# Two adjacency walks of a graph layer done as 2x2 blocks with seven products

## The chip, the cores and the metric

One core of one Trainium2 chip. The metric is the device time of one execution in microseconds; each kernel is given as the median of its runs. The profile is of one further execution, whose own time stands beside its span. Engine names in the profile: PE is TensorE (matmuls), PEld its loads of the stationary operand, DVE is VectorE, ACT is ScalarE, POOL is GpSimd, SP is SyncE, which here issues DMAs.

## The reference

Two graph layers over N = 2708 nodes with D = 256 features, all in float32; `adj` is a dense 2708 x 2708 matrix, mostly zeros. Only layer 0 matters for the change:

```python
R = adj + eye(N);  R = R / R.sum(-1, keepdims=True)
Xf = Xa = X;  Z = 0
for n in range(2):
    A  = top_p_attention(Xa, W1, W2, W3)   # softmax rows, cut at 0.9 of their mass
    Xf = R @ Xf
    Xa = A @ Xa
    Z  = Z + Xf @ U1[n].T + Xa @ U2[n].T
x = layernorm(X + layernorm(X + Z) * g + b)
```

Layer 1 is a graph attention with four heads over the mask `adj != 0`, a residual and a layer norm.

## The kernel before, in words

The rows are cut into 22 tiles (`rows`): 16 of 128 and 6 of 110. `adjT`, the transposed adjacency, lies in DRAM.

`fast_layer0` does layer 0. It has two attention steps (`step(0)`, `step(1)`) and two "walks", the products with R. By Horner's rule the walks run on projected features: `terms1` makes X U1[0].T (kept in DRAM as `c1`) and X U1[1].T (kept in SBUF as `xe`, with a column of ones for the row sums). Walk 0 multiplies R by `xe` and adds `c1`, giving `xm`; walk 1 multiplies R by `xm` and gives Xf's whole share of Z. The identity in R is added by VectorE when a row is done (`xf` at L931, `xw` at L990), not in the matrix.

One row of a walk is 22 matmuls (L917), one for each source tile j: the stationary operand is the 128 x 128 block of `adjT`, the moving one the 256 features (257 in walk 0) of the source tile, all summed in one PSUM bank (`ps_wk`, one buffer). The blocks come as half rows of 11 tiles (`blk`, three buffers in `adjp`, loaded two ahead by SP).

`step(s)` goes through the 22 row tiles of an attention step. For each row it has six groups of source tiles, and for each group one **slot**: four transposes of the score row `e` (`turned`, L256, into `ps_tr`, two buffers), ScalarE's copy (`eT`, L261), and four matmuls with the features (L274). The transposes of group n+1 stand before the matmuls of group n. After each group `slot(spend)` advances the searches for the cut of later rows (`going`: `scores`, `survey`, `bound`, `candidates`, `settle`, mostly VectorE and GpSimd; the last instruction of a search on VectorE is L851, the final `e`), then whatever finishes rows (`doing`), then the walks by `spend` matmuls:

```python
owed[0] += spend
while owed[0] > 0:
    owed[0] -= 1
    if next(stream, True):
        break
```

The search for row t + 3 is begun in the fifth slot of row t. In step 0 the spend is zero. Between the steps it is SPEND_BETWEEN per slot, 15 slots and those that `doing` needs, while the first searches of step 1 run; in step 1 it is SPEND_1. So walk 0 lies in the gap and the first part of step 1, walk 1 in the rest. All order is written out by hand (`manual_schedule`): each engine takes its instructions in program order, and waits on others by semaphores alone. `after_walk0` scales a row of walk 0 and adds `c1` (GpSimd); `finish` scales a row of walk 1, adds the other terms, and does two layer norms and layer 1's projections (`norms`, `sources`) in the slots that follow. Walk 1 waits in the program until no row of walk 0 is unfinished.

`layer1` follows: per source tile two loads of mask rows and features, VectorE's weights (`pt`, L1306) and TensorE's sums (L1318, L1328). `settle` there adds `xe`, the result of layer 0.

Of the kernel before, what the change touches and what calls it, by code (L numbers as in the profile page):

```python
# [8 lines left out]
F32 = mybir.dt.float32  # L9
# [27 lines left out]
SPEND_BETWEEN, SPEND_1 = 7, (7, 6, 7, 7, 6, 7)  # L37
# [8 lines left out]
def kernel(  # L46
# [55 lines left out]
    xe = const.tile([P, NT, D + 1], F32, name="xe")  # L102
    nc.gpsimd.memset(xe[:, :, D : D + 1], 1.0)
# [9 lines left out]
    vd = [kept.tile([P, D], F32, name=f"v_{t}") for t in range(NT)]  # L113
    bad = const.tile([1, 1], I32, name="bad")
# [41 lines left out]
    def sources(t, pool, room, queue=nc.sync):  # L156

        m = rows[t]
        tp = room()
        for c in range(DC):  # L160
            nc.tensor.transpose(tp[:, c, :m], xe[:m, t, c * P : (c + 1) * P], ident[:m, :m])
        xT = pool.tile([P, DC, P], F32, name="xT")
        nc.scalar.copy(xT[:, :, :m], tp[:, 0:DC, :m])
        yield
        wp = room().rearrange("p a b -> p (a b)")
        for c in range(DC):
            nc.tensor.matmul(  # L167
                wp[:m, : D + 2 * H], xT[:, c, :m], wx[:, c, :],
                start=(c == 0), stop=(c == DC - 1),
            )  # L170
        nc.scalar.activation(sb[:m, t, :], wp[:m, D : D + H], AF.Exp)
        nc.scalar.activation(tj[:m, t, :], wp[:m, D : D + H], AF.Exp, scale=NEG_SLOPE - 1.0)
        nc.scalar.copy(s_src[:m, t, :], wp[:m, D + H : D + 2 * H])
        vt = pool.tile([P, D], F32, name="cs")
        for h in range(H):
            cols = slice(h * FO, (h + 1) * FO)
            nc.scalar.activation(
                vt[:m, cols], wp[:m, cols], AF.Copy, scale=sb[:m, t, h : h + 1]
            )
        queue.dma_start(vd[t][:m], vt[:m])  # L180

    def norms(t, xt):

        m = rows[t]
        hh = xe[:m, t, 0:D]
        yield from layernorm(hh, hh, m)
        nc.gpsimd.tensor_mul(hh, hh, g_sb[:m])
        nc.gpsimd.tensor_add(hh, hh, xt[:m])
        yield
        yield from layernorm(hh, hh, m)  # L190
        yield
        yield
# [90 lines left out]
    def general_layer0():  # L283
        with ExitStack() as l0:
# [6 lines left out]
            load_x(xe)  # L291
            nc.scalar.dma_start(w1_sb, w1T.rearrange("(c p) e -> p c e", p=P))
# [248 lines left out]
    def fast_layer0(ep, adjp):  # L541
# [9 lines left out]
        )  # L551
        ps_lg, ps_wk, ps_at, ps_tr = (
            l0.enter_context(tc.tile_pool(name=name, bufs=bufs, space=PSUM))
            for name, bufs in (("ps_lg", 2), ("ps_wk", 1), ("ps_at", 1), ("ps_tr", 2))
# [66 lines left out]

        def query_weights():

            tr = ps_tr.tile([P, 4, P], F32, name="tr")
            for c in range(DC):
                nc.tensor.transpose(tr[:DA, c, :], w1_raw[:, c, :], ident)
            nc.vector.tensor_copy(w1_sb, tr[:DA, 0:DC, :])
            for c in range(DC):
                tr = ps_tr.tile([P, 4, P], F32, name="tr")
                nc.tensor.matmul(  # L630
                    tr[:, 0, :DA], w1_sb[:, c, :], w2_sb, start=True, stop=True
                )
                nc.vector.tensor_copy(wkqk[:, c, 1], tr[:, 0, :DA])
# [235 lines left out]

        def walks():  # L870

            queue = [
                (s, t, j0, j1)
                for s in range(STEPS) for t in range(NT) for j0, j1 in ((0, HT), (HT, NT))
            ]

            def load(s, t, j0, j1):  # L880
                m = rows[t]
                blk = adjp.tile([P, NT - HT, P], F32, name="blk")
                if (s, t) < (0, 2):

                    nc.gpsimd.memset(blk[:, :, 0:1], 0.0)
                by_tile(blk[:, :, :m], adjT[:, off[t] : off[t + 1]], j0, j1)
                return blk

            blocks = [load(*queue[0]), load(*queue[1])]
            yield  # L890
            for n, (s, t, j0, j1) in enumerate(queue):
                m = rows[t]
                cur, w = (xe, D + 1) if s == 0 else (xm, D)
                while s and unfinished:
                    yield True
                blk = blocks.pop(0)
                if n + 2 < len(queue):
                    blocks.append(load(*queue[n + 2]))
                if j0 == 0:
                    ac = ps_wk.tile([P, CHUNK], F32, name="walk")  # L900
                    if s and t >= NT - LATE:
                        ca = x_late[:, t - NT + LATE, :]
                        nc.gpsimd.memset(ca[:, 0:1], 0.0)
                    else:
                        ca = finp.tile([P, D], F32, name="ca", bufs=4)
                    if s:
                        cb = finp.tile([P, D], F32, name="cb")
                        nc.sync.dma_start(ca[:m], x[off[t] : off[t + 1], :])
                        nc.sync.dma_start(cb[:m], c2[t][:m])
                        if t in c3:  # L910
                            assert t in stored
                            held[t] = finp.tile([P, D], F32, name="cc")
                            nc.sync.dma_start(held[t][:m], c3[t][:m])
                    else:
                        nc.sync.dma_start(ca[:m], c1[t][:m])
                for j in range(j0, j1):
                    nc.tensor.matmul(  # L917
                        ac[:m, :w], blk[: rows[j], j - j0, :m], cur[: rows[j], j, 0:w],
                        start=(j == 0), stop=(j == NT - 1),
                    )  # L920
                    if j == NT - 1:
                        doing.append(after_walk0(t, ac, ca) if s == 0 else finish(t, ac, ca, cb))
                        next(doing[-1])
                    yield j == NT - 1

        def after_walk0(t, ac, ca):
            m = rows[t]
            unfinished.add(t)
            r = rinv[:m, t : t + 1]
            xf = rowp.tile([P, D + 1], F32, name="xf")  # L930
            nc.vector.tensor_add(xf[:m], ac[:m, : D + 1], xe[:m, t, :])  # L931
            nc.vector.reciprocal(r, xf[:m, D : D + 1])
            yield
            nc.gpsimd.tensor_scalar(xf[:m, :D], xf[:m, :D], r, None, op0=ALU.mult)
            nc.gpsimd.tensor_add(xm[:m, t, :], xf[:m, :D], ca[:m])
            unfinished.remove(t)
# [3 lines left out]
        def after_attention0(t, xa):  # L940
# [7 lines left out]
            tp = ps_tr.tile([P, 4, P], F32, name="tr")  # L948
            turn(xa, m, tp, nc.scalar.copy, xT)
            yield  # L950
            if t % 2:
                pj = ps_tr.tile([P, 4, P], F32, name="tr").rearrange("p a b -> p (a b)")
                project(1, off[t - 1], 2 * m, pj, both, nc.scalar.copy, nc.scalar.copy)
                yield
            terms2(t, xT)

        def terms1(t, xT):

            m = rows[t]
            cy = ps_tr.tile([P, 4, P], F32, name="tr").rearrange("p a b -> p (a b)")  # L960
# [7 lines left out]
            nc.scalar.copy(xe[:m, t, 0:D], cy[:m, D : 2 * D])  # L968
            nc.gpsimd.dma_start(c1[t][:m], cs[:m])

        def terms2(t, xT):

            m = rows[t]
            cy = ps_tr.tile([P, 4, P], F32, name="tr").rearrange("p a b -> p (a b)")
# [10 lines left out]
        def finish(t, ac, ca, cb):  # L985

            m = rows[t]
            xt = xe[:m, t, 0:D]
            xw = rowp.tile([P, D], F32, name="xw")[:m]
            nc.vector.tensor_add(xw, ac[:m, :D], xm[:m, t, :])  # L990
            yield
            nc.scalar.activation(xw, xw, AF.Copy, scale=rinv[:m, t : t + 1])
            while t not in held:
                yield
            nc.gpsimd.tensor_add(xt, ca[:m], cb[:m])
# [3 lines left out]
            if t < NT - LATE:  # L999
                yield  # L1000
                yield from norms(t, ca)
                yield from sources(t, rowp, lambda: ps_tr.tile([P, 4, P], F32, name="tr"))
# [3 lines left out]
        early = []  # L1006
        ready, held = {}, {}
        stream = walks()
# [7 lines left out]
        def slot(spend, begin=None):  # L1016
# [5 lines left out]
            advance(doing)  # L1022
            owed[0] += spend
# [5 lines left out]
        def step(s, cur, spend):  # L1029
            turned_first = None  # L1030
            for t in range(NT):
# [3 lines left out]
                if s == 0 and t == NT - 1:  # L1035
                    next(stream)
                if s and t == NT - 2:
                    share(0, ps_tr.tile([P, 4, P], F32, name="tr"))
# [4 lines left out]
                def between(n):  # L1043
# [11 lines left out]
                    if s and (t, n) == (NT - 1, len(groups) - 2):  # L1055

                        early.extend(neighbours(0, j, adjp) for j in first[:2])
                    slot(spend[n], (s, t + 3) if n == len(groups) - 2 else None)
# [55 lines left out]
        with tc.manual_schedule(engines=engines):  # L1114
            query_weights()
            ahead = turn_x(groups[0])
            for n in range(len(groups)):
# [3 lines left out]
                pj = ps_tr.tile([P, 4, P], F32, name="tr").rearrange("p a b -> p (a b)")  # L1121
# [9 lines left out]
            layer1_weights()  # L1131
            step(0, xm, [0] * len(groups))
# [80 lines left out]
    def layer1(ep, adjp, r=None, verdict=None, early=()):  # L1213
# [61 lines left out]

        if r is None:
# [92 lines left out]
        def beside(g, i):  # L1369
# [6 lines left out]
            for part in list(running):  # L1376
                if next(part, running) is running:
                    running.remove(part)
            if rest and i >= 2 and i % 2 == 0:
# [119 lines left out]
```

## Time and profile before

| | |
|---|---|
| median of 3 runs | 1572.68 us (1571.36 to 1573.06) |
| the profiled execution: time, span | 1571.97 us, 1570.2 us |
| granted TensorE clock | 0.994 |
| step 0 / gap / step 1 with walk 0 / step 1 with walk 1 | 71 to 441 / 441 to 515 / 515 to 808 / 808 to 1194 us |
| the walks' matmul records, L917 | 2 x 968, 447 us |
| the attention's, L274 | 2 x 968, 462 us |
| DMA | 128.40 MB, 82 GB/s on average |

A float32 matmul shows as two records. In the table of groups a row reads: line, engine, operation, output<-inputs, shapes, count | busy us, mean ns of one | idle time of the engine before them and what ended most of it. Matmul records overlap, so the mean of one is longer than its pace. In the list of waits a row reads: who waited <- for whom: us in total, times, longest.

### The profile page before, as it was taken

Reading aid. Unit: us, or ns where it says so; the run is one execution under the profiler, and the core shown is the slowest. Engines: PE = TensorE matmul, PEld = TensorE weight load, DVE = VectorE, ACT = ScalarE, POOL = GpSimd, SP = SyncE. Lnnn points to the kernel's source line nnn. Section 1 sums busy time; section 2 is a strip of 40 time slices with the busy share of each in tenths; the row PEclk is TensorE's granted clock in tenths of the full one; section 3 lists DMA queues with packets and bytes.
Section 4 is the critical chain, followed back from the end, with each engine's and each line's share of the span. In section 5 each row is a group of like instructions: output and inputs, shape, how many; then the busy total and the mean of one; then the engine's idle time right before and its main releaser. Section 6 shows DMA issues by size and latency. Waiting matters only on the chain.

```text
span 1570.2 us, 25877 instructions
## 1 busy us (share of the span) xinstructions
PE 1531.9 (98%) x9085; PEld 1034.5 (66%) x9085; DVE 1207.4 (77%) x3689; ACT 792.7 (50%) x1428; POOL 410.8 (26%) x853
## 2 busy tenths in 40 slices
PE   8999999999998999999999999999999999999995
PEld 4477777776776888887787788887778323333342
DVE  4686777677308876878769888888885898999995
ACT  3444444444345355555555556556552444456474
POOL 2200000001022122232224454534542120035143
PEclk9999999999999999999999999999999999999998
DMA  6100000000144343333334343333335335334331
GB/s 165 61 12 13 9 13 9 9 9 11 45 103 117 86 101 82 97 79 74 86 87 108 94 111 104 105 102 100 100 76 140 101 107 173 107 101 133 85 109 45
DMA packets 172501, 128.40 MB, mean 82 GB/s; under 512 B 44342, under 2 KB 161804, under 8 KB 172362
## 3 DMA queue, kind: packets, MB, share of 16 engines
q1 hardware_dynamic: 162553, 112.36, 27.2%
q0 software_dynamic: 3648, 9.26, 1.8%
q10 hardware_dynamic: 6161, 5.03, 1.0%
q8 instruction: 74, 1.21, 0.3%
q14 instruction: 65, 0.53, 0.1%
HBM read 111.78 MB, written 13.46 MB: 80 GB/s over the span
## 4 chain that ended last, share of the span: by engine, by line
PE 88%; DVE 7%; issue 1%; POOL 1%; ACT 1%; DMA 0%; ACTq 0%; DVEq 0%; POOLq 0%
PE att L274 25%; PE walk L917 24%; PE acc L1318 11%; PE lg L677 7%; PE tr L256 6%; PE acc L1328 6%; DVE pt L1306 3%; PE tr L962 2%; PE tr L976 2%; PE tr L647 1%; PE tr L167 1%; DVE scr L767 1%; DVE scr L848 0%; DVE cand L782 0%; DVE e L851 0%
## 5 line engine op out<-in xcount | busy, mean ns | idle before, releaser
L261 ACT COPY eT<-tr 128x512 f32<-128x512 f32 (+5 forms) x264 | 141.4, 536 | 280.9 <-PE tr L256 278.3
L702 ACT ACTIVATE junk<-e,minus,rth 128x2708 bf16<-128x2708 f32 (+1 forms) x88 | 232.9, 2646 | 36.1 <-POOL rth L734 35.2
L274 PE MATMUL att<-xm,eT 128*128 128x256 f32 (+3 forms) x968 | 230.9, 380 | 0.4 <-ACT xa L1047 0.4
L274 PE MATMUL att<-ba,eT 128*128 128x256 f32 (+3 forms) x968 | 230.9, 380 | 0.3 <-ACT eT L261 0.2
L917 PE MATMUL walk<-xe,blk 128*128 128x257 f32 (+3 forms) x968 | 225.3, 384 | 5.0 <-DVE xf L931 5.0
L917 PE MATMUL walk<-xm,blk 128*128 128x256 f32 (+3 forms) x968 | 222.0, 380 | 1.5 <-DVE xw L990 1.5
L1318 PE MATMUL acc<-pt,v 128*32 128x512 f32 (+3 forms) x2112 | 218.3, 543 | 4.1 <-DVE pt L1306 3.2
L917 PEld LDWEIGHTS walk<-xe,blk 128*128 128x128 f32 (+3 forms) x968 | 178.5, 187 | 50.3 <-issue 12.6
L917 PEld LDWEIGHTS walk<-xm,blk 128*128 128x128 f32 (+3 forms) x968 | 177.6, 186 | 35.1 <-issue 4.9
L1306 DVE SCALAR_TENSOR_TENSOR pt<-e,tj,blk 128x1024 f32<-128x1024 f32 (+3 forms) x176 | 184.3, 1112 | 11.8 <-PE att L274 8.7
L274 PEld LDWEIGHTS att<-xm,eT 128*128 128x128 f32 (+3 forms) x968 | 169.6, 186 | 22.1 <-ACT xa L1047 0.8
L274 PEld LDWEIGHTS att<-ba,eT 128*128 128x128 f32 (+3 forms) x968 | 169.5, 186 | 22.1 <-ACT eT L261 0.8
L681 ACT ACTIVATE e<-lg 128x1024 f32<-128x1024 f32 (+1 forms) x132 | 121.1, 922 | 110.5 <-PE lg L677 107.0
L1318 PEld LDWEIGHTS acc<-pt,v 128*32 128x32 f32 (+1 forms) x2112 | 68.9, 110 | 138.3 <-issue 110.5
L782 DVE MAX8 cand<-e 128x8 f32<-128x170 f32 (+1 forms) x352 | 89.6, 323 | 90.5 <-ACT e L681 90.4
L256 PEld LDWEIGHTS tr<-ident,e 128*128 128x128 f32 (+3 forms) x968 | 115.1, 138 | 56.3 <-issue 21.0
L256 PE MATMUL tr<-ident,e 128*128 128x128 f32 (+3 forms) x968 | 147.1, 271 | 0.7 <-ACT xe L968 0.3
L1328 PE MATMUL acc<-pt,sb 128*32 128x512 f32 (+3 forms) x1056 | 113.0, 542 | 0.0
L1306 DVE SCALAR_TENSOR_TENSOR pt<-r,tj,blk 128x1024 f32<-128x1024 f32 (+1 forms) x88 | 109.9, 1313 | 1.2 <-PE acc L1328 0.4
L237 ACT ACTIVATE blk<-blk 128x1024 f32<-128x1024 f32 (+3 forms) x66 | 63.3, 959 | 79.3 <-DMA blk<-in_adjT_dram 63.9
L782 DVE MAX8 cand<-scr 128x8 f32<-128x97 f32 (+1 forms) x616 | 102.2, 244 | 0.0
L931 DVE TENSOR_TENSOR xf<-walk,xe 128x257 f32<-128x257 f32 (+1 forms) x22 | 9.4, 426 | 110.9 <-PE walk L917 110.9
(235 smaller groups left out, 1959.3 us busy)
## 6 DMA issues: line engine op xcount, KB each, us to landing
blk<-in_adjT_dram SPq DMA_DIRECT2D x32, 704.0 KB
blk<-in_adjT_dram SPq DMA_DIRECT2D x32, 512.0 KB
blk<-in_adjT_dram SPq DMA_DIRECT2D x48, 330.0 KB
blk<-in_adjT_dram SPq DMA_DIRECT2D x32, 320.0 KB
blk<-in_adjT_dram SPq DMA_DIRECT2D x12, 605.0 KB
blk<-in_adjT_dram SPq DMA_DIRECT2D x12, 440.0 KB
blk<-in_adjT_dram SPq DMA_DIRECT2D x18, 283.6 KB
c<-cs POOLq DMA_DIRECT2D x32, 128.0 KB, 2.0
```

The lines of the kernel that those rows point to most:

```text
L237: nc.scalar.activation(bar, bar, AF.Sign)
L256: nc.tensor.transpose(tr[: rows[t], q, :m], e[:m, off[t] : off[t + 1]], ident[:m, :m])
L261: copy(eT[:k, : len(grp), :m], tr[:k, : len(grp), :m])
L274: nc.tensor.matmul(acc, eT[: rows[t], q, :m], value(t), start=(t == 0), stop=(t == NT - 1),)
L677: nc.tensor.matmul(lg[:m, h, :w], qT[part, cols], kT[s][part, c0 : c0 + w], start=True, stop=True,)
L681: nc.scalar.activation(halves[:m, :, c0 : c0 + w], lg[:m, :, :w], AF.Exp, accum_out=zp[:m, n : n + 1],)
L702: nc.scalar.activation(junk[:m], e[:m], func, scale=rth, bias=minus1[:m], accum_out=acc)
L782: nc.vector.max(cand[:, n, :], src[:m, n * size : min(N, (n + 1) * size)])
L917: nc.tensor.matmul(ac[:m, :w], blk[: rows[j], j - j0, :m], cur[: rows[j], j, 0:w], start=(j == 0), stop=(j == NT - 1),)
L1306: nc.vector.scalar_tensor_tensor(pt[:k, :gw], targets[g][h // 2][:k, h % 2, :gw], tj[:k, j, h : h + 1], bar, op0=ALU.max, op1=ALU.mult,)
L1318: nc.tensor.matmul(acc[h // 2][c][to : to + SIDE, :w], v[j][:k, h, o : o + SIDE], probs[n][h][:k, c0 : c0 + w], **at,)
L1328: nc.tensor.matmul(acc[2][c][h * SIDE : (h + 1) * SIDE, :w], sb[:k, j, h : h + 1].to_broadcast([k, SIDE]), probs[n][h][:k, c0 : c0 + w], **at,
```

## The change

Row tiles and source tiles are taken in pairs (11 of each, i and j), the features in halves of 128. In each pair of pairs the 2x2 block product is done with seven products instead of eight (Winograd's form of Strassen's scheme). On the side of the adjacency:

- S1 = A21 + A22, S2 = S1 - A11, S3 = A11 - A21, S4 = A12 - S2; D11 and D22 are A11 and A22, in which the identity is added into the diagonal block.

On the side of the features: T3 = B22 - B12, T2 = T3 + B11, T1 = B12 - B11, T4 = B21 - T2.

**Sums of the adjacency** (`mixes`): in step 0's slots, nine slots per row pair, 11 row pairs. SP loads the four blocks (each 11 x 128 x 128), GpSimd makes two diagonal adds and four sums in three pieces each, SP stores six blocks to DRAM. The fourth and fifth buffer are one tile of `wk`.

**The walks**: a row pair is seven phases of 11 matmuls with 128 moving columns (129 in the first three phases of walk 0); each phase's block is one load of 704 KB, two phases ahead. Two PSUM banks alternate, so `ps_tr` falls to one buffer, and the other small users of `ps_tr` take the banks of the walks before these begin and those of the scores (`lg`) afterwards (`free_bank`). After each phase the bank is read: p1 and the first half of row a by ScalarE, the other five by VectorE.

**Features**: T2, T3, T4 lie in the room of `xm`, T1 in the room of B12. Hence walk 0's result goes to DRAM (`xmd`) and comes back into `xe` at the end of the walk (`return_rows`), where the blends are made anew (`reblend`); walk 1 waits for that after its first phase. Since `xe` is then in use to the end, `finish` works in six lines of SBUF and stores to DRAM (`xd`), and layer 1 loads 19 tiles back once.

**Spend**: a phase's matmul is half as wide, so the spends are 14 and (12, 11, 11, 12, 11, 11). The walks' first load is issued at the end of step 0's last row.

```diff
-SPEND_BETWEEN, SPEND_1 = 7, (7, 6, 7, 7, 6, 7)
+SPEND_BETWEEN, SPEND_1 = 14, (12, 11, 11, 12, 11, 11)
...
-            for name, bufs in (("ps_lg", 2), ("ps_wk", 1), ("ps_at", 1), ("ps_tr", 2))
+            for name, bufs in (("ps_lg", 2), ("ps_wk", 1), ("ps_at", 1), ("ps_tr", 1))
...
+            for i in range(PAIRS):
+                m = rows[2 * i]
+                b11, b12, b21, b22, n = load(i)
+                yield
+                yield
+                yield
+                for key, b in (("D11", b11), ("D22", b22)):
+                    nc.gpsimd.tensor_add(b[:m, i, :], b[:m, i, :], ident[:m, :m])
+                    put(key, i, b)
+                count = 0
+                for key, dst, x0, x1, op in (
+                    ("S3", n, b11, b21, ALU.subtract),
+                    ("S1", b21, b21, b22, ALU.add),
+                    ("S2", b11, b21, b11, ALU.subtract),
+                    ("S4", b12, b12, b11, ALU.subtract),
+                ):
+                    for j0, j1, k in pieces_:
+                        at = (slice(0, k), slice(j0, j1), slice(None))
+                        nc.gpsimd.tensor_tensor(dst[at], x0[at], x1[at], op=op)
+                        count += 1
+                        if count % 2 == 0:
+                            if j1 == PAIRS:
+                                put(key, i, dst)
+                            yield
+                    if count % 2:
+                        put(key, i, dst)
...
+        PHASES = (
+            ("D11", "B11", 0, True), ("S2", "T2", 1, True), ("A12", "B21", 0, False),
+            ("S3", "T3", 1, False), ("S1", "T1", 0, True), ("D22", "T4", 1, True),
+            ("S4", "B22", 0, False),
+        )
...
-                while s and unfinished:
+                while s and (unfinished or (n and blending)):
                     yield True
...
+                if start:
+                    use[bank] = ps_wk.tile([P, CHUNK], F32, name=f"walk{(bank + i) % 2}")
...
+                for j in range(PAIRS):
+                    k = rows[2 * j]
                     nc.tensor.matmul(
-                        ac[:m, :w], blk[: rows[j], j - j0, :m], cur[: rows[j], j, 0:w],
-                        start=(j == 0), stop=(j == NT - 1),
-                    )
...
+                        ac, blk[:k, j, :], MOVING[name](j, k, w),
+                        start=start and j == 0, stop=j == PAIRS - 1, skip_group_check=True,
+                    )
+                    if j == PAIRS - 1:
+                        if n == 0:
+                            nc.scalar.copy(p1[:m, :w], ac)
+                        elif n == 1:
+                            nc.vector.tensor_add(y1[:m, :w], ac, p1[:m, :w])
...
+                        elif n == 2:
+                            nc.scalar.copy(xa[:m, :HALF], ac[:, :HALF])
...
+                        elif n == 3:
+                            nc.vector.tensor_add(y2[:m, :HALF], ac, p1[:m, :HALF])
+                        elif n == 4:
+                            nc.vector.tensor_add(xb[:m, HALF:], ac, y2[:m, :HALF])
+                        elif n == 5:
+                            nc.vector.tensor_add(xb[:m, :HALF], ac, y2[:m, :HALF])
+                        else:
+                            nc.vector.tensor_add(xa[:m, HALF:], ac, y1[:m, :HALF])
...
+            if begun:
+                next(mixing, None)
             owed[0] += spend
...
+            if fast and (g, i) == (0, 12):
+                for t0, t1 in ((0, 16), (16, NT - LATE)):
+                    nc.sync.dma_start(
+                        xe[: rows[t0], t0:t1, 0:D], xd[: rows[t0], t0:t1, :]
+                    )
```

## The prediction

> **What bounds the kernel now.** I read the page's busy shares first, then the windows of the stages, then the chain of waits for the pace of each kind of matmul.
>
> ```profile
> PE 1531.9 (98%) x9085; PEld 1034.5 (66%) x9085; DVE 1207.4 (77%) x3689; ACT 792.7 (50%) x1428; POOL 410.8 (26%) x853
> ```
>
> TensorE is busy in every stage; 0.2% of a run (some 3 us) is about the least that counts as a change here. The stages (columns: stretch, its length, busy us of PE, PEld, DVE, ACT, POOL with counts, clock, DMA share, GB/s):
>
> ```profile
> 71.50:441.00 369.50, 367.73 (x1855) 268.30 (x1853) 248.97 (x914) 158.21 (x357) 32.31 (x98) 1.00 0.06 17
> 441.00:515.00 74.00, 68.94 (x298) 52.85 (x299) 40.87 (x159) 36.26 (x44) 20.53 (x54) 0.98 0.43 107
> 515.00:808.00 293.00, 292.76 (x1433) 235.24 (x1432) 223.46 (x850) 157.31 (x199) 72.42 (x182) 1.00 0.35 86
> 808.00:1000.00 192.00, 190.84 (x940) 157.29 (x939) 161.10 (x605) 114.43 (x189) 85.38 (x169) 1.00 0.40 104
> 1000.00:1194.00 194.00, 193.31 (x963) 153.35 (x962) 167.44 (x635) 108.06 (x213) 88.51 (x173) 1.00 0.38 98
> ```
>
> These are: step 0's attention; the gap between steps; step 1 beside walk 0; step 1 beside walk 1 (two rows). PE is full throughout; GpSimd and the DMAs idle in the first; VectorE reaches 84 to 86% in the last two. A piece of the chain of waits gives the pace (start, us, what):
>
> ```profile
> 526.14 0.44 PE tr L256 x4
> 526.57 1.73 PE att L274 x8
> 528.30 3.04 PE walk L917 x14
> ```
>
> A float32 matmul leaves two records. Moving 256 or 257 columns takes 1.73/8 = 216 and 3.04/14 = 217 ns a record; a transpose that moves 128 takes 0.44/4 = 110. So the time follows the moving columns and the weight load (190 ns in its row) hides. Does it still hide behind 128 columns? One line has a shorter move behind full 128x128 weights: L647 with 74 columns. Its weight loads, from two narrow timelines (a load lasts 190 ns, so two spanning 0.30 us start 0.11 apart):
>
> ```profile
> 282.34 0.30 PEld L647 LDWEIGHTS tr<-xT,wkqk 128*128 128x128 f32 x2
> ...
> 282.45 0.30 PEld L647 LDWEIGHTS tr<-xT,wkqk 128*128 128x128 f32 x2
> ```
>
> Loads overlap each other and follow every 110 to 112 ns.
>
> **What the Trainium skill says.** "TensorE: Matmul & The Clock Gate", LDWEIGHTS: a load takes its columns / 1.2 ns, 107 for 128; the trace's 110 to 112 agrees. "SBUF — State Buffer", Who interferes with whom: a VectorE instruction with two SBUF inputs and a GpSimd instruction that reads SBUF exclude each other. The trace agrees: GpSimd's 128x256 add takes 0.73 us in L998 and 1.40 in L1256, beside layer 1's two-input VectorE work. "DMA: Bandwidth & Descriptors", Anatomy of one DMA: about 2 us fixed; the page's 2.0 us for c<-cs agrees.
>
> **The change, part by part.**
>
> 1. Walk matmuls. Before: 2 walks x 484 matmuls x 2 records, 968 at 217 and 968 at 216 ns: 419.2 us. After: 7 phases x 11 pairs x 11 source pairs = 847 matmuls a walk. In eight pairs the stationary has 128 columns, bound by the load at 112 ns; in three it has 110, bound by the move of 128 columns at 109. 1232 x 0.112 + 462 x 0.109 = 188.3 us a walk, 376.7 for both. **Gain 42.5 us.** The ideal eighth of 419 is 52; ten of it go to the weight load. Bounds: 109 throughout gives 50; 118 gives 20.
>
> 2. Block sums, in step 0. Per row pair: four fetches, twelve GpSimd pieces of 512 or 384 elements, two diagonal adds, six stores. GpSimd prices:
>
> ```profile
> L998 POOL TENSOR_TENSOR ca<-ca,b_sb 128x256 f32<-128x256 f32 x16 | 11.7, 732 | 0.0
> L689 POOL TENSOR_TENSOR fact<-fact,zp 128x1 f32<-128x1 f32 x32 | 7.3, 228 | 29.8 <-ACT e L681 28.7
> ```
>
> That is (732 - 228)/255 = 2.0 ns an element: 1.24 and 0.99 us a piece, 13.9 per pair and 1.0 for the diagonals: 15 us, 160 us in all, in a stage with 337 us of idle POOL. The chain of a pair: fetches. The page's main queue moved 162553 packets of 691 bytes in 27.2% of 16 engines' span, 42 ns each, 263 GB/s at full share: a 704 KB block takes 2.7 us, the third has landed after 2 + 8.2 = 10.2. Then 15 us of sums, and the next pair's fetch into the same buffer waits until S2's store has landed, 2 + 2.7 us after its last piece, of which S4's sums cover 3.5: 1.2 us more. VectorE's e (L851, 3.0 us, two SBUF inputs) shuts GpSimd out 1.5 times in that span: 2.6 us by GpSimd's share of 0.57. Period 26.5 to 29 us. The generator spends nine slots per pair; a tile takes 17.2 us in the trace, a slot 2.87, nine slots 25.8. So GpSimd falls behind by up to 8 x 3.2 = 26 us (the last three pairs are 14% smaller). Behind it on the POOL queue wait z and tau (L688 to L691), VectorE's settle, then PE. Tau is first read three slots later (8.6 us), and e was final 19.9 us before PE's first transpose of its tile: 28 us of cover. c2's stores and their two cs buffers have two tiles, 34 us. Also moved past on SP: nothing but the sums' own 220 transfers. I charge 2 us; bounds 0 and 25.
>
> 3. Evacuation. Per pair five VectorE adds of 128 columns replace two of 256 (L931: 426 ns). The nearest row of that width is L241, 281 ns: 1.4 us for 0.85, so +0.6 us a pair with the reciprocals, 13 us over 22 pairs. Two ScalarE copies a pair (0.3 us) lie in its 40% of idle time. Each bank is read one phase before it is written again, so no wait by itself.
>
> 4. Step 1's deadlines. Spend per tile is 68 matmuls for 40: 68 x 2 x 0.111 = 15.1 us for 40 x 0.433 = 17.3. Beside walk 1 VectorE does 328.5 us in 386; after, 328.5 + 7 + 3.5 for the blends = 339 in 365: 93%. Now the waits:
>
> ```profile
> DVE xf L931 <- PE walk L917: 110.9, 20, 44.5
> DVE xw L990 <- PE walk L917: 47.1, 18, 10.5
> ```
>
> VectorE's idle time is waiting for a row's end, that is, it runs ahead of PE. With an evacuation in five phases of seven (a phase is about a slot) it can't: the final e of a search, issued one slot before PE transposes it, then starts only after the slot's evacuation. In the trace e is ready 3.0 to 7.8 us ahead beside walk 1. A slot of 5.05 us less 3.1 for e leaves 2 us, less VectorE's backlog. No row shows such a stall, so I choose: 0.2 us for each of the nine tiles beside walk 0 and 0.85 for each of the thirteen beside walk 1, 13 us. Bounds: 2, if VectorE keeps its lead, and 30, if nearly all of the 2.2 us that a tile gains is lost beside walk 1.
>
> 5. Gap between steps. 252 matmuls at 0.222 for 126 at 0.433: 56 us for 54, so VectorE's first searches are covered as before. PE idled 5 us here (74.0 - 68.9) behind single-bank xf; now it waits at each phase behind bursts (28 maxima take 4.5 us) with a phase, 2.45 us, of slack. Blocks come at 704 KB per phase, 294 GB/s when contiguous, above the 263 of the mean packet; six of seven come in longer packets. Charge 3; bounds -4 and 8.
>
> 6. Between the walks, rows come back from DRAM (2 us and 2.7), then T3 and T2 on VectorE (2 x 1.8 by 1 ns an element): 8 us after the last phase, of which PE has a slot's attention and phase 0 to cover some 5. Charge 3; bounds 1 and 7.
>
> 7. At nothing: ps_tr with one buffer. The copy of one group's transposes ended 0.15 us or more before the next group's began, 7 of 263 times excepted (2.7 us in all if each waited). lg shared with projections: they lost ps_tr's competition for it. Blends at step 0's end hide behind its last tile. The first blocks of walk 0: SP's queue is free ahead. Layer 1's reload of 19 tiles, 2.4 MB or 9 us of DMA in front of mask loads that have two iterations of lead: charge 1.5, bounds 0 and 4.
>
> Sum: 42.5 - 2 - 13 - 3 - 3 - 1.5 = 20 us. The profiled execution took 1571.97 us (1570.2 of span and 1.8 around it), the median 1572.68: **1552 us**.
>
> **Rivals.**
> - All of it arrives: VectorE is still below PE in every stage, so the deadlines hold, and the charges shrink to 5: 1572 - 37 = 1535. For: 84% beside walk 0. Against: step 1's small lead. 0.22.
> - VectorE becomes the pace: of the 2.2 us that a tile gains, 1.6 are lost beside walk 1 and 0.7 beside walk 0, 13 x 1.6 + 9 x 0.7 = 27 us for the 13 charged: 1566. Against: 339 us of work would fit in 365. 0.13.
> - Slower: GpSimd's chain sets step 0. Eleven pairs in 99 slots have 284 us and 28 of cover. The sums' gain of 22 without this charge is gone at (284 + 28 + 22)/11 = 30.4 us a pair. If a piece costs a third more (L1256 shows 1.40 for 0.73) a period is 33 us, step 0 grows by 51, the time is 1601. For: 29 us is my upper sum; against: VectorE has two SBUF inputs in a fifth of step 0 only. 0.12.
> - The weight load doesn't hide, 190 ns a record: 3388 x 0.190 = 644 us, 225 more, near 1790. L647's 110 speaks against. 0.03.
> - That the blocks aren't the product, or the fallback runs, nothing suggests.
>
> **How the numbers follow.** The forecast, 1541 to 1564, has 0.50. Faster by over 0.2%: 0.50 + 0.22 + 0.08 of the VectorE case = 0.80; within: the other 0.05; slower: 0.12 + 0.03 = 0.15. The range goes from full gain with little charge, 1530, to VectorE's case at its worst, 1576, and leaves out the last two rivals.
>
> **What would show it.** Walk records x1694 a walk, at 109 to 112 ns; at 190 the base is wrong. Step 0 of 370 us; if longer, with DVE or PE waiting for tau, the third rival. Beside walk 1, PE's waits for DVE e and the evacuating adds, and a VectorE share of 90 to 93%. Blocks never waited for by PE after the gap.

## The result, and the profile after

| | before | after |
|---|---|---|
| median of 4 runs | 1572.20 us (1571.36 to 1573.06) | 1554.20 us (1553.71 to 1555.15) |
| the profiled execution: time, span | 1571.97, 1570.2 us | 1554.5, 1552.5 us |
| granted TensorE clock | 0.994 | 0.987 |

The ratio is 0.9886, 95% interval 0.9869 to 0.9903: the change saves 18.0 us. The forecast was 1552.

The page's busy shares come first: TensorE has lost 35 us of busy time and 2 points of its share, and VectorE has gained 90 us, far more than the change gives it to do (e3 below shows that most of it is waiting).

```profile
PE 1496.7 (96%) x10537; PEld 1068.9 (69%) x10537; DVE 1297.9 (84%) x3763; ACT 800.4 (52%) x1472; POOL 611.0 (39%) x1016
```

The stages, in the columns used before (stretch, length, busy us of PE, PEld, DVE, ACT, POOL with counts, clock, DMA share, GB/s): step 0, the gap, step 1 beside walk 0, and step 1 beside walk 1 in two rows.

```profile
71.00:441.00 370.00, 367.34 (x1853) 268.03 (x1854) 326.55 (x918) 158.06 (x357) 228.48 (x257) 1.00 0.70 215
441.00:521.00 80.00, 72.81 (x549) 65.35 (x548) 38.17 (x156) 37.34 (x51) 22.11 (x55) 0.94 0.66 199
521.00:790.00 269.00, 267.58 (x1899) 236.66 (x1898) 224.78 (x863) 159.41 (x209) 66.24 (x174) 1.00 0.54 163
790.00:1000.00 210.00, 203.84 (x1418) 180.71 (x1417) 189.12 (x709) 128.42 (x226) 105.20 (x200) 0.98 0.55 167
1000.00:1194.00 194.00, 184.21 (x1312) 161.89 (x1311) 161.04 (x607) 101.89 (x208) 75.60 (x149) 0.98 0.55 165
```

Step 0 is as long as before, though GpSimd now works there and VectorE shows 78 us more. In the gap and beside walk 1, and only there, PE's busy time falls clearly short of the length (by 7, 6 and 10 us) and the clock is below 1.00. Cut at the same instructions in both traces (the first matmul of each walk, the first transposes of a step, the last matmul of walk 1), and with the best kernel of the experiments beside them, the stages are:

| us | before | after | e12_best |
|---|---|---|---|
| step 0 | 369.8 | 370.6 | 370.5 |
| gap | 73.8 | 80.2 | 75.1 |
| step 1 beside walk 0 | 293.5 | 269.4 | 268.9 |
| from the start of walk 1 to its end | 404.5 | 406.3 | 394.8 |
| from there to the end | 357.1 | 355.6 | 356.4 |

Nearly all of the net gain lies beside walk 0. Walk 1, which saves as many matmuls, gained next to nothing. A part of this is only where the cuts fall among the attention's records: after has 396 of them beside walk 0 for 404, 544 beside walk 1 for 528, and 28 behind it for 36. Sixteen records with their transposes are some 4 us, so like for like walk 1 gained 2 us and walk 0's stage 22. The chain of waits beside walk 0 gives the pace (start, us, what):

```profile
527.49 0.44 PE tr L258 x4
527.93 1.73 PE att L276 x8
529.66 2.45 PE walk L1080 x22
```

A walk record takes 2.45/22 = 111 ns where it took 217, and the attention's 216 and the transposes' 110 are unchanged. Over whole walks, outside pauses and stretches of low clock, the mean from record to record went from 220.7 to 113.2 ns in walk 0 and from 217.1 to 112.1 in walk 1. The matmuls alone thus gained 968 x 0.2207 - 1694 x 0.1132 = 21.9 us and 968 x 0.2171 - 1694 x 0.1121 = 20.3 us. What became of more than half of these 42 us is in PE's waits from the start of step 1 to the end of walk 1 (waiting <- waited for: us, times, longest). Here `blk<-S` is the load of a block of sums, `xw` a row of a walk's result, `xe` the operand of the next walk, and `eT` ScalarE's copy of the transposes:

```profile
PE walk L1080 <- DMA blk<-S: 4.6, 1, 4.6
PE walk L1080 <- POOL xe L1151: 4.6, 1, 4.6
PE tr L258 <- ACT eT L263: 2.8, 3, 1.0
PE walk L1080 <- DVE xw L1098: 2.6, 2, 1.9
```

Five smaller ones add 2.7 us. The same view of before held 1.5 us for `xw` and two other waits of 0.3 and 0.2 us. The gap has two waits of its own for a block:

```profile
PE walk L1080 <- DMA blk<-S: 6.3, 2, 4.1
```

None of the pauses over 2 us is for VectorE's deadlines. In each, what PE waits for stood in the queue of an engine that was itself waiting for something else.

**Gap.** SP's waits there (SPq is SP issuing a transfer):

```profile
SPq L1149 <- POOL xw L1148: 9.0, 3, 3.8
```

SP stood 9 us in all at three stores of finished rows of walk 0, for which GpSimd was late. Behind the last of them stood three block loads.

**Handover.** The chain of waits at the start of walk 1:

```profile
790.26 0.65 POOL c L1272
...
792.53 0.94 POOL xw L1146
...
793.55 1.32 POOL xe L1151
...
796.82 0.73 POOL xe L1151
...
797.60 2.93 PE walk L1080 x12
```

GpSimd's queue was held until 790.3 by a store (L1272) whose data ScalarE had only just written. Behind it stood six small operations of a search and then the last two rows of walk 0, which PE needed. PE resumed at 797.6 after a pause of 4.6 us.

**End of walk 1.** SP's waits from 1150 us on, and the piece of the chain before PE's last long pause:

```profile
SPq L1049 <- POOL x_late L1042: 8.2, 1, 8.2
```

```profile
1179.38 10.41 DMA blk<-S
```

SP stood 8.2 us at a load into `x_late`, for a one-element write by GpSimd that stood behind a layer norm. The last two blocks came after it on SP, the last one behind two broadcasts as well.

**Clock.** The records of the granted clock show half speed for 3.4 or 6.8 us at a time, beginning close to the end of such a pause, from 2.4 us ahead of it to 0.7 behind: 3.4 us at 474, 6.8 at 498, 795 and 1188 (and 3.4 at 1208, in layer 1). Before had one of 3.4 us at 507. Half of what lies behind the pause is lost, as the last line of the chain at the handover shows (2.93/12 = 244 ns a record for 111): 4.2 us in the gap (1.7 before), 2.2 at the handover, 2.3 at the end.

"TensorE: Matmul & The Clock Gate" of the Trainium skill, What's actually happening, has free-running windows of 3413 ns and half rate after at least one idle window. The records agree with the window: in each of the fourteen traces of this case all beginnings and ends between 430 and 1530 us lie on one grid of 3413 ns, which falls differently in each trace. They do not agree with the condition. In the thirteen traces other than e2's, PE had no record running for 1.78 us or more of each of the 48 windows that half speed followed, and for 1.78 us or less of 4072 of the 4073 that full speed followed. Half speed went on after windows with 0.66 us or more of idle (19) and ended after those with 0.63 or less (46). So a pause of some 2 us draws half speed as a rule if it lies in one window, and may draw none if the grid divides it.

### The profile page after: what moved, and what is told of

It is laid out like the page before. It is cut to its first block, busy times and chain, and to the rows that moved or that the text cites. A ratio compares the mean times of both kernels' runs of the same rounds, so it can differ in the third digit from the quotient of the medians.

```text
span 1552.5 us, 29929 instructions
## 1 busy us (share of the span) xinstructions
PE 1496.7 (96%) x10537; PEld 1068.9 (69%) x10537; DVE 1297.9 (84%) x3763; ACT 800.4 (52%) x1472; POOL 611.0 (39%) x1016
## 4 chain that ended last, share of the span: by engine, by line
PE 83%; DVE 8%; POOL 3%; ACT 2%; DMA 2%; issue 2%; ACTq 0%; DVEq 0%; SPq 0%; POOLq 0%
PE att L276 24%; PE walk L1080 20%; PE acc L1552 11%; PE lg L783 7%; PE tr L258 6%; PE acc L1562 6%; DVE pt L1540 3%; PE walk L1181 2%; PE walk L1197 2%; DMA blk<-S 1%; PE walk L753 1%; PE lg L170 1%; DVE top L906 1%; DVE work L908 1%; ACT junk L808 1%
## 5 line engine op out<-in xcount | busy, mean ns | idle before, releaser
L1080 PE MATMUL walk<-xe,blk 128*128 128x128 f32 (+7 forms) x1936 | 242.4, 277 | 12.5 <-DMA blk<-S 4.6
L1080 PEld LDWEIGHTS walk<-xe,blk 128*128 128x128 f32 (+3 forms) x1936 | 230.7, 188 | 28.6 <-issue 16.8
L1080 PE MATMUL walk<-xm,blk 128*128 128x128 f32 (+6 forms) x1452 | 188.0, 280 | 7.8 <-DMA blk<-S 6.3
L888 DVE MAX8 cand<-e 128x8 f32<-128x170 f32 (+1 forms) x352 | 85.8, 323 | 20.4 <-ACT e L787 20.3
L906 DVE MAX8 top<-work 128x8 f32<-128x128 f32 (+3 forms) x242 | 82.4, 340 | 8.3
```

Source lines behind the costliest of these rows:

```text
L888: nc.vector.max(cand[:, n, :], src[:m, n * size : min(N, (n + 1) * size)])
L906: nc.vector.max(top[:, k : k + 8], work if k else flat)
L1080: nc.tensor.matmul(ac, blk[:k, j, :], MOVING[name](j, k, w), start=start and j == 0, stop=j == PAIRS - 1, skip_group_check=True,)
```

## The experiments

Kernels e1 to e8 were timed against before at 1572.1 us, e9 to e12 at 1571.75. Ratios are to before. Line numbers of experiments can differ by one or two from those of after.

**e1_halves: half the width in the kernel before.** Each matmul of a walk is split into two halves of the moving columns, same stationary block.

```diff
+                    for c0, c1_ in ((0, w // 2), (w // 2, w)):
-                        ac[:m, :w], blk[: rows[j], j - j0, :m], cur[: rows[j], j, 0:w],
+                        ac[:m, c0:c1_], blk[: rows[j], j - j0, :m], cur[: rows[j], j, c0:c1_],
```

> The kernel before, with each walk matmul split into two halves of the features (128 or 129 moving columns) on the same block; all eight products, no sums, nothing else changed. Theory: the weight load sets 112 ns a record with 128 stationary columns and the move 109 with 110, 3872 records, 430 us for 419: about 1583. Rival 1, the halved move costs nothing beyond its columns (108.5 ns): 1573. Rival 2, the load does not hide (190 ns a record): near 1890.

Measured: 1581.73 us, ratio 1.0061 (1.0044 to 1.0077). The chain beside walk 0:

```profile
528.05 1.73 PE att L274 x8
529.78 3.12 PE walk L918 x28
```

3.12/28 = 111 ns a record, with none of the change's other parts present. Twice the records cost 9.5 us over two walks: half width is nearly half price, and the price of a record in the prediction is confirmed. Contrary to the expectation's wording, not all sums survive in this kernel, though every product is issued: the two halves each begin a sum in the same bank, and what is lost there was not traced. It is read for its pace alone.

**e2_narrow: is it the load or the move?** Only 64 of the 128 columns move, except in a bank's first matmul; the rest of each product is left out.

```diff
-                        ac, blk[:k, j, :], MOVING[name](j, k, w),
+                        ac[:, v:], blk[:k, j, :], MOVING[name](j, k, w)[:, v:w],
```

> The changed kernel with 64 moving columns instead of 128 in all matmuls of a phase but the first of a bank; half of the sums over features is left out. Theory: the weight load is the bound, so 128-column blocks keep 112 ns and only the 110-column blocks go from 109 to about 97: 11 us less than 1554, 1543. Rival, the move sets the pace: 54 ns less for nearly all of 3388 records, about 176 us less, 1380.

Measured: 1551.0 us (1548.5 to 1559.0), ratio 0.9861 (0.9845 to 0.9878). A stretch at full clock:

```profile
541.43 2.63 PE walk L1081 x24
```

2.63/24 = 110 ns a record for half of the columns. Over both walks, with 128 stationary columns the median spacing stays at 112 ns, and with 110 it falls from 109 to 97. So the weight load sets the pace of a full block, and the rival of 1380 us is out. "TensorE: Matmul & The Clock Gate", LDWEIGHTS, gives columns / 1.2 ns, 107 and 92 for these two; 112 and 97 lie 5 ns above both. The time missed both the 1543 and the 1380, and what held it up neither side had named. The window of the gap:

```profile
441.00:540.00 99.00, 95.51 (x563) 84.82 (x563) 41.93 (x169) 39.01 (x54) 26.25 (x57) 0.72 0.53 167
```

The clock is 0.72. It was at half for 54.6 us from 473.4 on, 16 windows of 3413 ns, although PE was busy almost throughout; one pause, of 2.3 us, lies at the beginning. The gap took 95.5 us for 80.2, while the stages beside the two walks fell by 7.7 and 4.3 us, together about the gain that was expected. This is the slowest of the four executions, and the others had a somewhat higher clock (0.975 to 0.978 for 0.970).

**e3_nosums: the block sums without GpSimd.** The twelve GpSimd pieces per pair are left out; loads, diagonals and stores stay.

```diff
-                        nc.gpsimd.tensor_tensor(dst[at], x0[at], x1[at], op=op)
```

> The changed kernel without the twelve GpSimd sums per pair; loads, diagonal adds and stores stay, so the walks read plain blocks. Theory: the sums are hidden in step 0, so the time stays within 3 us of 1554, while VectorE's busy time in step 0 falls from 327 to about 250 us. Rival, the sums hold step 0 up through tau: 10 to 25 us less, 1530 to 1544.

Measured: 1555.96 us, ratio 0.9893 (0.9876 to 0.9909). Step 0 took 371.2 us for 370.6; most of what the profiled execution took more than after lies behind the last matmul, in an ending of 21.0 us for 18.5. VectorE's row for step 0 shows what the sums do:

```profile
70.00:441.00 371.00, 368.22 (x1857) 268.28 (x1856) 254.32 (x918) 158.12 (x358) 53.25 (x125) 1.00 0.70 215
```

254.3 us for 326.6 with the sums. The groups of step 0 say where the 72 us are, first of e3, then of after:

```profile
L909 DVE TENSOR_TENSOR_SCAN sums<-top 128x56 f32<-128x56 f32 (+1 forms) x20 | 5.5, 274 | 0.7
L956 DVE SCALAR_TENSOR_TENSOR e<-e,fact 128x2708 f32<-128x2708 f32 (+1 forms) x20 | 60.7, 3034 | 0.0
```

```profile
L910 DVE TENSOR_TENSOR_SCAN sums<-top 128x56 f32<-128x56 f32 (+1 forms) x20 | 69.8, 3489 | 0.7
L957 DVE SCALAR_TENSOR_TENSOR e<-e,fact 128x2708 f32<-128x2708 f32 (+1 forms) x20 | 68.6, 3431 | 0.0
```

A scan (a running sum along a row) of 0.27 us shows as 3.5 on average, its longest as 10.1, and without GpSimd's pieces it is 0.27 again. It is the first VectorE instruction of a search that streams two inputs from SBUF. "SBUF — State Buffer", Who interferes with whom, has the two engines exclude each other for whole instructions. The trace agrees, and goes further: the longest scan lasted as long as eight pieces of 1.0 to 1.3 us that followed each other almost without a break. The prediction had GpSimd waiting for VectorE. In fact VectorE waits out a run of GpSimd pieces. It had 120 us to spare in this stage, so the sums cost at most 0.8 us.

**e4_evac: VectorE's deadlines.** The five evacuating adds by VectorE become copies by ScalarE; the sums with p1, y1 and y2 are left out.

```diff
-                            nc.vector.tensor_add(y1[:m, :w], ac, p1[:m, :w])
+                            nc.scalar.copy(y1[:m, :w], ac)
```

> The changed kernel with the five VectorE adds that read the walks' banks replaced by ScalarE copies; the addends p1, y1, y2 are left out. Theory (the lost time is in three stalls of PE behind SP's and GpSimd's queues): PE's few waits for these adds and for the final e go, 2 to 4 us less than 1554, 1551. Rival, as predicted (VectorE's deadlines in step 1 take 13 us): 10 to 13 us less, 1542.

Measured: 1552.62 us, ratio 0.9876 (0.9859 to 0.9892). Walk 1's stage fell from 406.3 to 404.9 us. PE's waits in step 1:

```profile
PE walk L1080 <- POOL xe L1151: 4.8, 1, 4.8
PE walk L1080 <- DMA blk<-D: 3.9, 3, 1.9
PE walk L1080 <- DMA blk<-S: 2.2, 1, 2.2
```

The waits for VectorE's adds and two of the three for `eT` are gone, and waits for blocks took part of their place; in the gap a wait of 3.0 us for one of the new copies came in. In the median the kernel is 1.6 us faster than after, within its spread (1550.1 to 1555.5). Without these adds walk 1's stage is still as long as before's 404.5. So the charge of 13 us for deadlines is refuted, as is the VectorE rival, by this time and by PE's waits in after, 2.9 us for all adds in step 1.

**e5_xmd and e10_hold: SP's queue in the gap.** Two ways to keep the `xmd` store from blocking the loads: on GpSimd's queue, or on SP's but a slot later.

```diff
-                nc.sync.dma_start(xmd[:m, t], xw)
+                nc.gpsimd.dma_start(xmd[:m, t], xw)
```

> The changed kernel with walk 0's results stored to DRAM by GpSimd's own queue instead of SP's, so that no block load stands behind such a store. Theory: the two stalls in the gap (2.3 and 4.3 us) and the half-speed clock after them (3.4 us each way) go: about 9 us less than 1554, 1545. Rival, VectorE's first searches set the end of the gap anyway: at most 3 us less, 1551.

Measured: 1556.62 us, ratio 0.9902 (0.9885 to 0.9918). The gap shrank to 77.9 us and its half speed went. PE's waits for blocks in it fell from 6.3 to 0.9 us, but PE now waited 7.3 us for VectorE there, 3.1 at the longest, much as the rival had it for the gap. Why VectorE was later is not shown; GpSimd's stores now stand between its small operations for the searches. And after the last matmul the program took 22.6 us to end instead of 18.5, so the time missed both expectations. The cause of these 4.1 us is open; they came again in e8, the other kernel with these stores on GpSimd. Of the kernels with them on SP only e3 had a longer ending, by 2.4 us.

```diff
                 nc.gpsimd.tensor_add(xw, xw, ca[:m])
+                yield
                 nc.sync.dma_start(xmd[:m, t], xw)
```

> The store of a finished row of walk 0 (xmd, L1149) stays on SP's queue but is issued a slot later in the program, when GpSimd's add is done. Theory (in the gap SP stood at that store while GpSimd was behind, with three block loads after it): the gap's stalls of 2.3 and 4.3 us and its half clock shrink, the gap falls from 80.2 to 76 to 78 us, nothing is added at the end, and the time is 1550 to 1552. Rival (the blocks of the gap are late because DMA itself is short there): gap within 1 us of 80, 1553 to 1556.

Measured: 1549.27 us (4 runs), ratio 0.9856 (0.9841 to 0.9871). The gap took 75.0 us. PE's waits for an S block there:

```profile
PE walk L1080 <- DMA blk<-S: 2.5, 2, 2.2
```

2.5 us for 6.3: after the store SP issued the next block at 492.1 where it had been 495.5. SP still stood at these stores, 11.0 us for 9.0 in all, but the block was no longer behind the second of two. DMA was not short; the order on SP was. Of the 5.2 us that the gap lost, some 2.5 are half speed (3.4 us of it for 10.2). The gaps of e7 and e9, which their edits do not touch, have as little of it and take 77.6 and 78.1 us, so about 3 us are left for the edit itself.

**e6_hand: GpSimd's queue at the handover.** The last two rows of walk 0 are scaled and added by one VectorE instruction each.

```diff
-            nc.gpsimd.tensor_scalar(xw, xw, rinv[:m, t : t + 1], None, op0=ALU.mult)
-                nc.gpsimd.tensor_add(
+                nc.vector.scalar_tensor_tensor(
```

> The changed kernel with the last two rows of walk 0 scaled and added by one VectorE instruction each instead of two GpSimd instructions each. Theory: PE's 4.8 us at the start of walk 1 are GpSimd's queue (a store that waits for attention, z and tau stand ahead), so they go, with 3.4 us of half-speed clock: 6 to 8 us less, 1547. Rival, the rows' way back from DRAM and the blends are as late: PE waits in the next phase instead, 0 to 2 us less.

Measured: 1553.47 us (1551.7 to 1556.4), ratio 0.9888 (0.9872 to 0.9905). PE's waits from 780 to 812 us:

```profile
PE walk L1080 <- DVE xm L1000: 1.9, 1, 1.9
PE walk L1080 <- DVE xe L1151: 0.5, 1, 0.5
```

The wait for GpSimd's `xe` is gone. The blend for the next phase is late instead, for 1.9 us. Walk 1's stage fell by 2.9 us to 403.4; in the median of whole runs only 0.7 us of it shows, within the spread. That is the rival's case.

**e7_spread: the broadcasts at the end.** The broadcasts of layer 1 are issued three slots later.

```diff
-                    spread(0, ahead)
...
+                        spread(0, ahead)
                         early.extend(neighbours(0, j, adjp) for j in first[:2])
```

> The changed kernel with layer 1's four broadcast loads (e<-shared, 2 MB) issued three slots later, after the walk's block loads. Theory: the last 4.8 us stall of walk 1 is a block load behind these broadcasts, and goes with 3.4 us of half-speed clock: 6 to 8 us less, 1547. Rival, layer 1 then waits for the broadcasts: the stall only moves, 1552 to 1558.

Measured: 1554.17 us, ratio 0.9884 (0.9867 to 0.9901). The pause of 4.6 us stayed, at 4.3, and so did this wait of SP:

```profile
SPq L1049 <- POOL x_late L1042: 8.2, 1, 8.2
```

The edit did not bring the broadcasts behind the last block, so it decides nothing on them. What it leaves is that SP stood before both, the broadcasts and the block.

**e8_all3: e5, e6 and e7 together.**

> The three edits together (stores of walk 0 on GpSimd's queue, the handover by VectorE, the broadcasts later). Theory: the gains add, 20 to 24 us less than 1554, about 1532. Rival, the next thing is as late (VectorE's deadlines): 8 to 12 us less, 1544.

Measured: 1553.28 us, ratio 0.9878 (0.9862 to 0.9895). Gap 77.7, walk 1's stage 402.9 us, and 4.1 us given back in e5's longer ending. The gains did not add, and both expectations were missed.

**e9_late: SP's queue at the end.** The write into `x_late` is made once at the start of the kernel.

```diff
     x_late = const.tile([P, LATE, D], F32, name="x_late")
+    nc.gpsimd.memset(x_late[:, :, 0:1], 0.0)
...
-                    nc.gpsimd.memset(ca[:, 0:1], 0.0)
```

> The end of walk 1 in the trace of after: SP stood 8.2 us, from 1168 to 1176.3, at a load into x_late (L1049) that waits for a one-element write by GpSimd (L1042), and this stood in GpSimd's queue behind a norm (L138, L189, L190). Behind the load on SP stood the last two blocks. Here that write is made once at the start of the kernel. Theory (SP's order, not the broadcasts, is what makes the last blocks late): the S4 block is issued some 5 us or more earlier, PE's waits of 0.8 and 4.6 us and most of the 6.8 us at half clock at 1199 go, and the time is 1546 to 1548 (1554.2 for after). Rival (the two e<-shared broadcasts ahead of it are what makes the block land 10.4 us after its issue): the block still lands behind them, a stall of 3 us or more stays, 1552 to 1555.

Measured: 1547.84 us, ratio 0.9847 (0.9834 to 0.9861). Walk 1's stage fell from 406.3 to 401.4 us. PE waited 0.3 us for the last block. SP's longest wait from 1150 us on, and the block's way in the chain:

```profile
SPq L682 <- PE walk L1080: 9.6, 4, 3.7
```

```profile
1178.10 8.28 DMA blk<-S
```

SP now waits for the buffer, that is, it is as early as three buffers allow: the load leaves 0.2 us after PE begins the phase that frees the buffer, where it had been 3.5. The size of that step was expected larger (5 us); the other 2.1 us came from a shorter way. The gap took 78.1 us with the same two pauses as after, since they drew 3.4 us of half speed instead of 10.2: the first one, of 2.2 us, lay across an edge of the grid and drew none. The edit does not touch the gap, so these 2 us of the gain are not its own.

**e11_hand_late and e12_best: together.** e11 is e6 with e9; e12 adds e10.

> The write to x_late at the start, and the last two rows of walk 0 scaled and added by VectorE (as in e6). Theory: the two gains add, 3 us in the stage beside walk 1 from the handover (which the trace of e6 showed) and 6 to 8 from the end of the walk: 1543 to 1546. Rival (the end stall stays with the broadcasts): 1551 to 1554.

Measured: 1545.67 us, ratio 0.9833 (0.9820 to 0.9847); walk 1's stage 398.4 us.

> The three together: the write to x_late at the start, the last two rows of walk 0 by VectorE, the xmd stores a slot later. Theory (each of the three stalls is a store or load that stands on SP or GpSimd for another engine): gap 77, step 1 beside walk 1 395 to 399, 1541 to 1544. Rival (time comes back elsewhere, as DMA or VectorE is the next bound): 1548 or more.

Measured: 1539.95 us (1538.8 to 1544.6), ratio 0.9806 (0.9793 to 0.9820): 31.8 us less than before, and 14.3 less than the median of the change alone (12.6 by the two ratios). Its windows:

```profile
71.00:441.00 370.00, 367.80 (x1855) 268.09 (x1853) 324.62 (x918) 157.89 (x357) 229.95 (x257) 1.00 0.70 215
441.00:516.00 75.00, 70.44 (x543) 62.67 (x544) 37.46 (x153) 37.72 (x52) 23.16 (x54) 0.98 0.71 214
516.00:785.00 269.00, 268.02 (x1905) 237.31 (x1903) 225.24 (x867) 159.32 (x209) 67.04 (x175) 1.00 0.53 163
785.00:1180.00 395.00, 386.22 (x2740) 340.32 (x2737) 350.60 (x1319) 231.18 (x435) 177.12 (x342) 1.00 0.56 169
```

VectorE does as much beside walk 1 as in after (350.6 us) in 11 us less time, at 89%, and the clock is back at 1.00. Three edits that only put work elsewhere brought back about half of the 25 us that had been lost.

## Why the prediction was right, and where its steps failed

The sum was right within 2 us, the mechanism of the gain was right, and the losses were right in total and wrong in place. That the total came out is luck: one charge was 11 us too large, and four others, two of them taken at nothing, were together 17 us too small. In us of the profiled executions, less what before had of the same:

| step | charged | measured |
|---|---|---|
| 1 matmuls | gain 42.5 | gain 42.2 |
| 2 sums in step 0 | 2 | 0.8 |
| 3, 4 evacuation and VectorE's deadlines | 13 | 1.6 |
| 5 gap | 3 | 4.6: pauses +2.1, half clock +2.5 |
| 6 between the walks | 3 | 6.8: pause 4.6, half clock 2.2 |
| 7 one `ps_tr` buffer, shared `lg` | 0 | 3.7 |
| 7 layer 1's reload | 1.5 | none seen: PE's idle time behind the walks -0.4 |
| blocks at the end of walk 1 | 0 | 7.7: pauses 5.4, half clock 2.3 |
| ahead of step 0 | 0 | -1.1 |

The last row is chance, since step 0 began between 70.4 and 71.9 us in all fourteen traces. The measured charges sum to 23.7, and 42.2 - 23.7 = 18.5 us for the span's 17.7.

- **Step 1** held: e1 shows the record's price without the change, e2 that the load sets it for full blocks.
- **Step 2** held, through slack that the prediction did not use. It priced the lock as GpSimd's loss, and the trace shows it as VectorE's: 78 us, in a stage where VectorE had the time. GpSimd's own busy time there grew by 196 us for the 160 estimated. The slack was nearly used up: in most tiles of step 0 `e` was ready 19.9 us before PE's first transpose of it, as the prediction says, and after the change 2.3 us at the least. The third rival was closer than the 0.8 us suggest.
- **Step 4** failed. It argued that a search's last `e` would be late since VectorE must take part in five phases of seven. PE waited for no `e`: the least lead at a tile's first transpose beside walk 1 was 1.1 us. VectorE's share was 90% in the first half of the stage and 83% in the second, and its busy time there came to 350 us for the 339 estimated. Yet PE's waits for its adds sum to 2.9 us, for 1.5 in before: VectorE kept enough of its lead, the case for which the prediction's lower bound of 2 stood.
- **Steps 5 and 6** stayed within their bounds and were mis-sized for one reason. They counted transfers and VectorE's work (with a block as 704 KB; it is two loads, 677 KB in all), and did not ask what stands ahead of a block load on SP or of a row on GpSimd. The sentence "Blocks never waited for by PE after the gap" is refuted by the 4.6 us wait for an S block. e6, e9 and e10 each removed or shortened one such wait without changing what is computed or moved, and their gains add in e12 (e6's 2.9 us of its stage show as 2.2 between e9 and e11).
- **Step 7's ps_tr**: two pauses of 1.0 us, at 917 and 1110, are transposes waiting for ScalarE's copy, held up by a 2.65 us pass over `e` on ScalarE; a third of 0.7 is at the first group of step 1. The prediction had priced this at up to 2.7 us and then taken nothing. Another 1.4 us are small matmuls of layer 1 (L164, L170), which now wait for a bank of the scores; this was taken at nothing as well.
- **The charge nobody made** is the clock: 7 us net of half speed behind pauses. The handover's pause of 4.6 us cost 6.8. How much a pause draws depends on where the grid of windows falls, so 2 to 3 us of a kernel's gap are chance.
- **Rivals.** "All of it arrives" (1535) did not happen, though e12 at 1540 shows most of it was to be had. VectorE as the pace is excluded by e4, GpSimd's chain in step 0 by e3, and a weight load that does not hide by e1.

What stays open: the longer endings of e5, e8 and e3; the 0.8 us by which the account misses; why 54.6 us at half clock went on in e2; and what to do about the 8.5 us of pauses that e12 has left beside walk 1, of which 4.6 are waits for VectorE's blends and adds and 2.1 for ScalarE's copies.

## What to carry to other kernels

When work is made cheaper on the bounding engine, its operands must arrive at the new pace: list for each load what stands ahead of it on its in-order queue and which engine that waits for. Such a wait is cheap to remove (a store issued a slot later, a one-element write made at the start, a row moved to another engine), and three of them were worth some 13 us where the whole change was worth 18. Count a pause of TensorE of some 2 us or more as longer than it is, since half speed can follow it.

## What the runs showed of the hardware that was not expected

- A VectorE scan with two SBUF inputs went from 274 ns to 3489 ns on average, 10.1 us at the longest, beside back-to-back GpSimd additions, eight of which passed in those 10.1 us; VectorE's busy time in the profile holds the wait.
- With 64 moving columns TensorE stayed at half clock for 54.6 us while nearly always busy, in the one execution profiled; with 128 columns no stretch before the program's end was longer than 6.8 us. Windows without idle, which end half clock in the point below, did not end it here.
- A stationary block of 128 columns sets 112 ns for a record of a float32 matmul whether 64 or 128 columns move; 110 columns and 64 moving take 97 ns.
- Half speed followed the windows of 3413 ns in which TensorE was idle for 1.78 us or more (48 of 48 in thirteen traces; one with 2.02 us, in e9, it did not follow), and ended after one with 0.63 us or less. The same pause of 4.1 to 4.5 us drew 6.8 us of half speed in after and 3.4 in e9, and one of 2.1 to 2.2 us drew 3.4 and none.
- In both kernels with 20 stores moved from SP's to GpSimd's queue the end of the program was 4.1 us longer.
